# Cross-attention on one core: Wq and Wk in 512-byte runs turned by VectorE, the product G over 64 rows, and the first group's A in two halves

## The chip, the cores and the metric

The kernel runs on one core of one Trainium2 chip. The metric is the device time of one execution in microseconds. Four runs of the kernel before took 289.02 to 289.76 us, median 289.47.

## The reference

Sixteen images of 256 tokens attend to sixteen texts of 77 tokens, with 8 heads of 256 columns; everything is float32.

```python
# x (16,256,256), c (16,77,192); Wq (256,2048), Wk and Wv (192,2048), Wo (2048,256)
Q, K, V = heads(x @ Wq), heads(c @ Wk), heads(c @ Wv)
score = Q @ K.T / sqrt(256)           # masked keys get -inf
ctx = softmax(score) @ V
out = merge(ctx) @ Wo + x
y = (out - mean(out)) * rsqrt(var(out) + eps) * gamma + beta
```

## The kernel before, in words

The kernel never forms Q, K or V. For each head it multiplies the weights first: G = Wk·Wqᵀ (192 by 256) and U = Wv·Wo (192 by 256). The scores of an image are then x·A with A = Gᵀ·cᵀ, and the values are c·U. The 192 rows of c and of G are kept as 128 rows (cA, gA) and 64 rows (cB, gB, stored on both halves of the partitions, so that two matmuls over 64 rows can run on the two halves of TensorE's rows).

The order is written out by hand: the five engines each run their instructions in the order in which the program lists them. Loads go through SP's queue; the order of the program gives every load after the eighth a wait for the load eight before it. Up to the first scores the stages on TensorE are:

- ten idle transposes (L467), then the 22 transposes of ctx (`c_sb`, 11 blocks of 112 rows) at L475, evacuated in turn by ScalarE and VectorE (`evacuate`, L133 to L138) into cA and cB, with a copy of cB by GpSimd (L486). `vr` is set to zero at L490.
- for each of 8 heads: four transposes of Wq and four of Wk (L507, tiles p_wqT and p_wkT), evacuated to wqT and wkT, and then G (pg, L543): two matmuls over 128 rows, each of them two instructions in the profile, scaled into gA by L551. The transposes of head h+1 are issued ahead of G of head h.
- after four heads the last 64 rows of G for two pairs of heads (ph, L524), scaled into gB (L532, L534).
- A of the first group of four images (`prepare_a(0, ...)`), in two halves of four heads after all of G: part A with cA (L182), part B with cB (L196); in the second half part B comes ahead. Each half fills all eight PSUM banks. VectorE turns Wv in place meanwhile (L568).
- U (pu, L584, over 64 rows in pairs; pw, L602), then the values of the last 13 keys of all images (pr, L256 and L266).
- the scores of the first image (ps, L295), and from there a loop over the images.

The loads on SP come in this order: ctx in three pieces (L442); for each head a piece of Wq and of Wk (L445, L446), 256 columns of each row, so runs of 1024 bytes; Wv in sixteen loads (L454), each of 32 partitions with runs of 512 bytes from rows 8192 bytes apart; Wo (L456), whose tile takes the place of Wq's; the mask (L457); x in 256-byte runs to be turned (xT, L153, turned at L160); and x itself (xg, L129), whose tiles take the place of wqT and wkT. At L348 VectorE turns 32 by 32 blocks of the probabilities out of place.

Of the kernel before, what the change touches and what calls it, by code (L numbers as in the profile page):

```python
# [15 lines left out]
P = 128  # L16
# [28 lines left out]
def kernel(  # L45
# [16 lines left out]
    LP = DL // 2  # L62
# [34 lines left out]
    gA = const.tile([P, H, DI], F32, tag="gA", name="gA")  # L97
    gB = const.tile([P, NF, DI], F32, tag="gB", name="gB")
# [25 lines left out]
    def half(i):  # L124
        return slice(i * LB, (i + 1) * LB)
# [39 lines left out]
    def prepare_a(g, pairs, B_first=False):  # L165


        if 0 in pairs:
            a_of[g] = in_two("a", [P, 2, GB, H, S2], g)
        parts = [(2 * n + i, dc) for n in pairs for dc in range(2) for i in range(2)]  # L170
# [19 lines left out]
        def part_B():  # L190
            if B_first:
                banks.extend(ring_of(parts))
            for j in range(0, len(parts), 2):
                for i in range(NM):
                    for k, (h, dc) in enumerate(parts[j : j + 2]):
                        nc.tensor.matmul(  # L196
                            flat(banks[j + k][i * BK : (i + 1) * BK]),
                            gB[half(k), h // 2, cols(dc, i)],
                            flat(cB[half(k), batches, :]),
                            start=B_first,  # L200
                            stop=not B_first,
                        )
# [229 lines left out]
    with tc.tile_pool(name="wonce", bufs=1) as wp:  # L432
        c_sb = wp.tile([CR, NCR, DL], F32, tag="c", name="c_sb")
        wq_r = wq.rearrange("(t p) f -> p t f", p=P)
        wk_r = wk.rearrange("(t p) f -> p t f", p=LP)

        warm = wp.tile([P, 1], F32, tag="warm", name="warm")
        nc.scalar.activation(warm, eps, AF.Exp)
        wq_all = wp.tile([P, NF, 2, 2 * D], F32, tag="w128", name="wq_all")
        wk_all = wp.tile([LP, NF, 2, 2 * D], F32, tag="w96", name="wk_all")  # L440
        for lo, hi in ((0, 2), (2, 6), (6, NCR)):
            nc.sync.dma_start(c_sb[:, lo:hi, :], c_rows[:, lo:hi, :])  # L442
        for h in range(H):
            here, cols = slice(h % 2 * D, (h % 2 + 1) * D), slice(h * D, (h + 1) * D)
            nc.sync.dma_start(wq_all[:, h // 2, :, here], wq_r[:, :, cols])  # L445
            nc.sync.dma_start(wk_all[:, h // 2, :, here], wk_r[:, :, cols])  # L446
# [17 lines left out]

        def keep_busy(n):
            for i in range(n):
                nc.tensor.transpose(idle, ident, ident)  # L467

        keep_busy(10)
        for r in range(0, NCR, 2):  # L470
            n = min(2, NCR - r)
            pc = ps_mm.tile([P, 4, P], F32, tag="mm", name=f"pc_{r}")
            for lc in range(2):
                for j in range(n):
                    nc.tensor.transpose(  # L475
                        pc[:, 2 * lc + j, :CR],
                        c_sb[:, r + j, lc * LB : lc * LB + P],
                        ident[:CR, :CR],
                    )
            rows = slice(r * CR, (r + n) * CR)  # L480
            evacuate(flat(cA)[:, rows].rearrange("p (j m) -> p j m", m=CR), pc[:, :n, :CR])
            evacuate(
                flat(cB)[LB:, rows].rearrange("p (j m) -> p j m", m=CR),
                pc[LB:, 2 : 2 + n, :CR],
            )
            nc.gpsimd.tensor_copy(flat(cB)[:LB, rows], flat(cB)[LB:, rows])  # L486
        nc.gpsimd.tensor_copy(cRA, cA[:, :, KM:])
        nc.gpsimd.tensor_copy(cRB, cB[:, :, KM:])

        nc.gpsimd.memset(vr, 0.0)  # L490
# [3 lines left out]
            const.tile([P, H // 2, 2, DI], F32, tag=f"xg{i}", name=f"wqT_{i}") for i in range(2)  # L494
        ]
        wkT_of = [
            const.tile([P, H // 2, 2, DL], F32, tag=f"xg{i + 2}", name=f"wkT_{i}") for i in range(2)
        ]
        wqT = [wqT_of[h * 2 // H][:, h % (H // 2)] for h in range(H)]
        wkT = [wkT_of[h * 2 // H][:, h % (H // 2)] for h in range(H)]  # L500

        def turn_weight(dst, w_all, rows, h, tag):
            pt = ps_mm.tile([P, 4, P], F32, tag="mm", name=f"p_{tag}_{h}")
            for dc in range(2):
                for r in range(2):
                    lo = h % 2 * D + dc * P
                    nc.tensor.transpose(  # L507
                        pt[:, 2 * dc + r, :rows],
                        w_all[:, h // 2, r, lo : lo + P],
                        ident[:rows, :rows],  # L510
                    )
            evacuate(dst.rearrange("p a (r n) -> p (a r) n", r=2), pt[:, :, :rows])

        def turn_qk(h):
            turn_weight(wqT[h], wq_all, P, h, "wqT")
            turn_weight(wkT[h], wk_all, LP, h, "wkT")

        def rest_of_g(pairs):

            for n in pairs:  # L520
                pg = ps_mm.tile([P, DI], F32, tag="mm", name=f"ph_{n}")
                for dc in range(2):
                    for i in range(2):
                        nc.tensor.matmul(  # L524
                            pg[half(i)],
                            wkT[2 * n + i][:, dc, P:],
                            wqT[2 * n + i][:, dc, :],
                            start=(dc == 0),
                            stop=(dc == 1),
                        )  # L530
                if n % 2:
                    nc.scalar.mul(gB[:, n, :], pg, D ** -0.5)  # L532
                else:
                    nc.vector.tensor_scalar(gB[:, n, :], pg, D ** -0.5, None, ALU.mult)  # L534

        turn_qk(0)
        for h in range(H):
            if h + 1 < H:
                turn_qk(h + 1)
            if h % 2 == 0:  # L540
                pg = ps_mm.tile([P, 2, DI], F32, tag="mm", name=f"pg_{h}")
            for dc in range(2):
                nc.tensor.matmul(  # L543
                    pg[:, h % 2, :],
                    wkT[h][:, dc, :P],
                    wqT[h][:, dc, :],
                    start=(dc == 0),
                    stop=(dc == 1),
                )
            if h % 2:  # L550
                nc.scalar.mul(gA[:, h - 1 : h + 1, :], pg, D ** -0.5)  # L551
            if h % (H // 2) == H // 2 - 1:
                rest_of_g(range((h - 2) // 2, (h + 1) // 2))
        for g in range(NG):
            load_x(g)
            if g == 0:
                nc.sync.dma_start(gam, gamma.partition_broadcast(P))
                nc.sync.dma_start(bet, beta.partition_broadcast(P))

        for n in range(0, NF, 2):  # L560
            part_A, part_B, copies = prepare_a(0, (n, n + 1), B_first=(n > 0))
            for part in (part_A, part_B)[:: -1 if n else 1]:
                part()
            for dst, src in copies():
                evacuate(dst, src)
            for a in range(n, n + 2):
                blocks = wvT[:, a].rearrange("p m (c n) -> p m n c", n=4)
                nc.vector.transpose(blocks, blocks)  # L568
# [5 lines left out]


        def wv_part(a, e, n):
            return flat(wvT[half(e), a]).rearrange("p (l n) -> p n l", n=4)[:, n]

        for a in range(NF):
            if a % 2 == 0:  # L580
                pu = [ps_mm.tile([P, 2, DI], F32, tag="mm", name=f"pu_{a}_{e}") for e in range(2)]
            for n in range(4):
                for e in range(2):
                    nc.tensor.matmul(  # L584
                        pu[e][:, a % 2, :],
                        wv_part(a, e, n)[:, :P],
                        wo_all[half(e), a, n, :],
                        start=(n == 0),
                        stop=(n == 3),
                    )  # L590
            if a % 2:
                for e in range(2):
                    evacuate(
                        uA[:, e, :, a - 1 : a + 1].rearrange("p n a c -> p a n c"),
                        pu[e].rearrange("p a (n c) -> p a n c", c=BK),
                    )
        for pair in range(0, NF, 2):
            pw = [ps_mm.tile([P, DI], F32, tag="mm", name=f"pw_{pair}_{e}") for e in range(2)]
            for n in range(4):
                for i in range(2):  # L600
                    for e in range(2):
                        nc.tensor.matmul(  # L602
                            pw[e][half(i)],
                            wv_part(pair + i, e, n)[:, P:],
# [124 lines left out]
```

## Time and profile before

| | |
|---|---|
| median of four runs | 289.47 us |
| the profiled execution | 289.28 us |
| its span, first to last instruction | 287.1 us |
| start of the first scores (L295) | 60.45 us |
| TensorE busy, share of the span | 278.1 us, 97% |
| VectorE, ScalarE, GpSimd busy | 212.9, 118.6, 119.5 us |
| moved by DMA | 22.50 MB |

A row of digits in the profile cuts the span into 40 slices of 7.2 us; a digit is the busy share of a slice in tenths. The chain of work that ended last is followed back from the last instruction; each of its pieces has a start, a length and a source. Stretches of time show the busy time of each engine, the clock granted to TensorE, the mean busy share of the 16 DMA engines, and GB/s.

### The profile page before, as it was taken

How to read it: one execution, taken by the hardware profiler on the slowest of the kernel's cores; microseconds unless marked ns; L12 is line 12 of the kernel's file. 1: busy time of each engine (PE TensorE's matmuls, PEld its weight loads, DVE VectorE, ACT ScalarE, POOL GpSimd, SP SyncE). 2: the span in 40 equal slices, each digit the busy share in tenths (PEclk: the TensorE clock that was granted, in tenths of full speed). 3: DMA queues.
4: the chain of work that ended last, by engine and by line, in shares of the span. 5: the costliest groups of instructions: out<-in, count | busy, mean ns of one | idle time of the engine just before them, and what ended most of it. 6: DMA issues, size and time to landing. Idle time of an engine off the chain costs nothing.

```text
span 287.1 us, 11524 instructions
## 1 busy us (share of the span) xinstructions
PE 278.1 (97%) x5216; PEld 184.1 (64%) x5216; DVE 212.9 (74%) x419; ACT 118.6 (41%) x205; POOL 119.5 (42%) x150
## 2 busy tenths in 40 slices
PE   7999999999999999999999999999999999999990
PEld 6976569894666565656575757575757467576550
DVE  1422482765858798989797989897979898898884
ACT  3443222123253535353535353535353534635541
POOL 2700060804534334343334342434342527658584
PEclk9999999999999999999999999999999999999997
DMA  7998999990000101910101019000000000010112
GB/s 201 263 247 223 338 178 286 300 130 8 2 3 2 40 5 38 149 39 2 39 6 39 2 36 151 31 13 25 16 21 23 15 28 17 24 41 1 41 39 73
DMA packets 34673, 22.50 MB, mean 78 GB/s; under 512 B 17648, under 2 KB 33984, under 8 KB 34624
## 3 DMA queue, kind: packets, MB, share of 16 engines
q1 hardware_dynamic: 34624, 21.77, 32.7%
q8 instruction: 41, 0.67, 1.0%
q14 instruction: 8, 0.07, 0.1%
HBM read 17.57 MB, written 4.19 MB: 76 GB/s over the span
## 4 chain that ended last, share of the span: by engine, by line
PE 92%; DMA 2%; DVE 2%; POOL 2%; ACT 0%; issue 0%; POOLq 0%; SPq 0%
PE ps L295 23%; PE po L360 22%; PE pa L182 12%; PE pv L223 10%; PE pa L196 6%; PE pv L234 6%; PE pu L584 3%; PE pg L543 3%; PE pr L256 2%; DMA c_sb<-in_ctx_dram 2%; PE p_wqT L507 1%; PE ph L524 1%; PE pw L602 1%; PE pr L266 1%; PE p_wkT L507 1%; PE pc L475 1%
## 5 line engine op out<-in xcount | busy, mean ns | idle before, releaser
L317 POOL TENSOR_TENSOR s<-s,top 128x616 f32<-128x616 f32 x32 | 39.0, 1218 | 90.8 <-DVE top L316 86.4
L295 PE MATMUL ps<-a,xT 128*32 128x154 f32 x2048 | 70.0, 294 | 0.0
L295 PEld LDWEIGHTS ps<-a,xT 128*32 128x32 f32 x2048 | 66.4, 110 | 3.6 <-issue 0.8
L338 POOL TENSOR_TENSOR p<-e,rden 128x512 f32<-128x512 f32 x64 | 50.1, 802 | 31.8 <-ACT a L667 27.0
L360 PE MATMUL po<-vw,pT 128*32 128x256 f32 x1024 | 61.5, 380 | 0.0
L360 PEld LDWEIGHTS po<-vw,pT 128*32 128x32 f32 x1024 | 31.7, 110 | 28.2 <-issue 5.5
L330 DVE TENSOR_REDUCE den<-e 128x8 f32<-128x616 f32 x32 | 25.3, 790 | 23.7 <-ACT e L324 23.7
L182 PE MATMUL pa<-cA,gA 128*32 128x308 f32 x512 | 35.8, 423 | 0.0
L324 ACT ACTIVATE e<-s 128x616 f32<-128x616 f32 x32 | 23.0, 718 | 28.8 <-POOL s L317 28.7
L665 ACT COPY vw<-pv 128x512 f32<-128x512 f32 x32 | 18.6, 581 | 36.1 <-PE pv L234 36.1
L309 DVE TENSOR_TENSOR s<-ps,bias 128x308 f32<-128x308 f32 x64 | 27.8, 465 | 4.1 <-PE ps L295 4.1
L223 PE MATMUL pv<-uA,cA 128*32 128x512 f32 x256 | 30.4, 592 | 0.0
L182 PEld LDWEIGHTS pa<-cA,gA 128*32 128x32 f32 x512 | 16.4, 110 | 21.0 <-issue 6.6
L417 DVE SCALAR_TENSOR_TENSOR xg<-xg,rstd,bet 128x256 f32<-128x256 f32 x25 | 27.9, 1116 | 0.9
L385 ACT ACTIVATE std<-mv,eps 128x2 f32<-128x2 f32 (+1 forms) x17 | 5.0, 296 | 55.0 <-DVE mv L377 54.3
L348 DVE STREAM_TRANSPOSE pT<-p 128x640 f32<-128x640 f32 x32 | 25.0, 810 | 2.5 <-POOL p L338 2.5
L316 DVE TENSOR_REDUCE top<-s 128x8 f32<-128x616 f32 x32 | 25.4, 795 | 1.1
L360 PE MATMUL po<-vr,pT 128*32 128x256 f32 x256 | 19.7, 379 | 0.0
L385 ACT ACT_TABLE_LOAD x15 | 19.2, 1283 | 0.3
L196 PE MATMUL pa<-cB,gB 64*32 64x308 f32 x512 | 19.3, 419 | 0.0
L324 ACT ACT_TABLE_LOAD x14 | 18.0, 1283 | 0.2
L234 PE MATMUL pv<-uB,cB 64*32 64x512 f32 x256 | 17.4, 601 | 0.0
(73 smaller groups left out, 284.5 us busy)
## 6 DMA issues: line engine op xcount, KB each, us to landing
xT<-in_x_dram SPq DMA_DIRECT2D x16, 256.0 KB, 6.7
xg<-in_x_dram SPq DMA_DIRECT2D x4, 1024.0 KB, 11.4
out_dram<-xg SPq DMA_DIRECT2D x15, 256.0 KB, 2.3
wq_all<-in_L_xattn_Wq_dram SPq DMA_DIRECT2D x8, 256.0 KB, 6.9
wo_all<-in_L_xattn_Wo_dram SPq DMA_DIRECT2D x4, 512.0 KB, 5.5
wk_all<-in_L_xattn_Wk_dram SPq DMA_DIRECT2D x8, 192.0 KB, 6.9
wvT<-in_L_xattn_Wv_dram SPq DMA_DIRECT2D x16, 96.0 KB, 3.0
bias<-in_mask_BxS_if_dram SPq DMA_DIRECT2D x1, 616.0 KB, 9.7
```

Source lines behind the costliest of these rows:

```text
L182: nc.tensor.matmul(flat(o[i * BK : (i + 1) * BK]), gA[:, h, cols(dc, i)], flat(cA[:, batches, :]), start=not B_first, stop=B_first,)
L196: nc.tensor.matmul(flat(banks[j + k][i * BK : (i + 1) * BK]), gB[half(k), h // 2, cols(dc, i)], flat(cB[half(k), batches, :]), start=B_fir ...
L223: nc.tensor.matmul(pv[k][i * BK : (i + 1) * BK], cA[:, b, k * BK : (k + 1) * BK], uA[:, :, :, i], start=True, stop=False,)
L234: nc.tensor.matmul(pv[k][i * BK : (i + 1) * BK], cB[half(k), b, k * BK : (k + 1) * BK], uB[half(k), :, :, i], start=False, stop=True,)
L295: nc.tensor.matmul(ps[m // 2][i * BK : (i + 1) * BK, m % 2 * 2 * S2 : (m % 2 + 1) * 2 * S2], xT_of[g][:, j * NM + m, dc], flat(a_of[g][:, ...
L309: nc.vector.tensor_tensor(s[:, a * H // 2 : (a + 1) * H // 2], ps[a][:, : H // 2 * S2].rearrange("p (h k) -> p h k", k=S2), bias[:, b, :]. ...
L316: nc.vector.tensor_reduce(top, s, AX.X, ALU.max)
L317: nc.gpsimd.tensor_tensor(s, s, top.unsqueeze(2).to_broadcast([P, H, S2]), ALU.subtract)
L324: nc.scalar.activation(e, s_of.pop(t), AF.Exp)
L338: nc.gpsimd.tensor_tensor(part, e_mh[:, :, :, keys], rden_mh.unsqueeze(3).to_broadcast(list(part.shape)), ALU.mult,)
L360: nc.tensor.matmul(po[i * BK : (i + 1) * BK], pT[:, n, i], vw_of[b][:, n // 2, n % 2, :] if n < NF else vr[:, b, :], start=(n == 0), stop= ...
L417: nc.vector.scalar_tensor_tensor(y, y, rstd, bet, ALU.mult, ALU.add)
```

## The change

Wq and Wk come in four blocks of two heads. Each block is eight loads of 32 partitions with runs of 512 bytes, in the form that Wv has already: partition 32·i + r holds, for each 32-row block m of the weight, row r of column piece i. Wk of the first block is issued on ScalarE's queue, ahead of its table load, all others on SP. The first three blocks of ctx are loaded after two blocks of weights, the other eight after all four.

VectorE turns each block of 32 by 32 out of place (eight instructions in all), and the result holds 64 columns of one head on each half of the partitions for each of four steps n. TensorE has no transposes of Wq and Wk. G runs over 64 rows, two heads at once on the two halves, through functions that U shares: `of_pair` for the first 128 rows of G or U, `rest_of_pairs` for the last 64. gB has a new order of heads, and `prepare_a` picks its heads to match.

The order on TensorE becomes: 28 idle transposes; G of block 0; 6 transposes of ctx; G of block 1 and the rest of G for both; A of the first four heads; the other 16 transposes of ctx; G of blocks 2 and 3; A of the other heads, now with part A ahead in both halves; then U as before. The loads of x (xg) and gamma and beta are listed after the second part of G, in the same place on SP's queue as before, behind xT.

```diff
-        parts = [(2 * n + i, dc) for n in pairs for dc in range(2) for i in range(2)]
+        parts = [
+            (u // 2 * 4 + 2 * i + u % 2, dc) for u in places for dc in range(2) for i in range(2)
+        ]
...
-                            gB[half(k), h // 2, cols(dc, i)],
+                            gB[half(k), h // 4 * 2 + h % 2, cols(dc, i)],
...
+        wq_nat = wp.tile([P, NF, DI // BK, P], F32, tag="w128", name="wq_nat")
+        wk_nat = wp.tile([P, NF, NL, P], F32, tag="w96", name="wk_nat")
+        wq_blocks = wq.rearrange("(m r) (a i f) -> a i r m f", r=BK, a=NF, i=NM)
+        wk_blocks = wk.rearrange("(m r) (a i f) -> a i r m f", r=BK, a=NF, i=NM)
+
+        def load_qk(a, queues):
+            for queue, nat, blocks in zip(queues, (wk_nat, wq_nat), (wk_blocks, wq_blocks)):
+                for i in range(NM):
+                    queue.dma_start(nat[i * BK : (i + 1) * BK, a], blocks[a, i])
...
+        first = -(-GB * S2 // CR)
+        load_qk(0, (nc.scalar, nc.sync))
...
-        for lo, hi in ((0, 2), (2, 6), (6, NCR)):
-            nc.sync.dma_start(c_sb[:, lo:hi, :], c_rows[:, lo:hi, :])
-        for h in range(H):
-            here, cols = slice(h % 2 * D, (h % 2 + 1) * D), slice(h * D, (h + 1) * D)
-            nc.sync.dma_start(wq_all[:, h // 2, :, here], wq_r[:, :, cols])
-            nc.sync.dma_start(wk_all[:, h // 2, :, here], wk_r[:, :, cols])
+        load_qk(1, (nc.sync, nc.sync))
+        load_c(0, first)
+        load_qk(2, (nc.sync, nc.sync))
+        load_qk(3, (nc.sync, nc.sync))
+        load_c(first, NCR)
...
-        keep_busy(10)
+        for i in range(28):
+            nc.tensor.transpose(idle, ident, ident)
...
+        def turn_qk(a):
+            for nat, of in ((wk_nat, wkT_of), (wq_nat, wqT_of)):
+                nc.vector.transpose(
+                    of[a // 2][:, a % 2].rearrange("p n (m r) -> p m n r", r=BK),
+                    nat[:, a].rearrange("p m (n c) -> p m n c", c=BK),
+                )
...
+        def of_pair(out, a, weight, moving):
+
             for n in range(4):
                 for e in range(2):
                     nc.tensor.matmul(
+                        out[e][:, a % 2, :],
+                        weight(a, e, n)[:, :P],
+                        moving(a, e, n),
                         start=(n == 0),
                         stop=(n == 3),
                     )
...
+        turn_qk(0)
+        turn_qk(1)
+        for j in range(NF // 2):
+            pg = two_banks("pg", j)
+            of_pair(pg, 2 * j, wk_part, wq_part)
+            if j == 0:
+                turn_c(0, first)
+            of_pair(pg, 2 * j + 1, wk_part, wq_part)
             for e in range(2):
+                nc.scalar.mul(gA_of[:, j, e], pg[e], D ** -0.5)
+            for e, ph in enumerate(rest_of_pairs(j, wk_part, wq_part, "ph")):
+                nc.vector.tensor_scalar(gB[:, 2 * j + e, :], ph, D ** -0.5, None, ALU.mult)
+            if j == 0:
+                turn_qk(2)
+            else:
+                turn_v(0)
+                turn_v(1)
+                for g in range(NG):
+                    load_x(g)
...
+            part_A, part_B, copies = prepare_a(0, (2 * j, 2 * j + 1))
+            part_A()
+            part_B()
+            for i, (dst, src) in enumerate(copies()):
+                evacuate(dst, src)
+                if j == 0 and i == 3:
+                    turn_qk(3)
+            if j == 0:
+                turn_c(first, NCR)
+                nc.gpsimd.tensor_copy(cRA, cA[:, :, KM:])
+                nc.gpsimd.tensor_copy(cRB, cB[:, :, KM:])
+                nc.gpsimd.memset(vr, 0.0)
+        turn_v(2)
+        turn_v(3)
```

More of the change, by code (lines that the diff above doesn't have):

```diff
@@ L61 @@
     S2, DL = c.shape[1], c.shape[2]
-    LP = DL // 2
     LB = DL - P
@@ L160, in transpose_x, with prepare_a @@
         nc.vector.transpose(cols, cols)
-    def prepare_a(g, pairs, B_first=False):
-        if 0 in pairs:
+    def prepare_a(g, places, B_first=False):
+        if 0 in places:
             a_of[g] = in_two("a", [P, 2, GB, H, S2], g)
-        parts = [(2 * n + i, dc) for n in pairs for dc in range(2) for i in range(2)]
+        parts = [
+            (u // 2 * 4 + 2 * i + u % 2, dc) for u in places for dc in range(2) for i in range(2)
+        ]
         batches = slice(g * GB, (g + 1) * GB)
@@ L433, with load_c @@
         c_sb = wp.tile([CR, NCR, DL], F32, tag="c", name="c_sb")
-        wq_r = wq.rearrange("(t p) f -> p t f", p=P)
-        wk_r = wk.rearrange("(t p) f -> p t f", p=LP)
+        wq_nat = wp.tile([P, NF, DI // BK, P], F32, tag="w128", name="wq_nat")
[6 more added lines that the diff above has]
+                    queue.dma_start(nat[i * BK : (i + 1) * BK, a], blocks[a, i])
+        def load_c(lo, hi):
+            nc.sync.dma_start(c_sb[:, lo:hi, :], c_rows[:, lo:hi, :])
+        first = -(-GB * S2 // CR)
+        load_qk(0, (nc.scalar, nc.sync))
         warm = wp.tile([P, 1], F32, tag="warm", name="warm")
         nc.scalar.activation(warm, eps, AF.Exp)
-        wq_all = wp.tile([P, NF, 2, 2 * D], F32, tag="w128", name="wq_all")
-        wk_all = wp.tile([LP, NF, 2, 2 * D], F32, tag="w96", name="wk_all")
-        for lo, hi in ((0, 2), (2, 6), (6, NCR)):
-            nc.sync.dma_start(c_sb[:, lo:hi, :], c_rows[:, lo:hi, :])
-        for h in range(H):
-            here, cols = slice(h % 2 * D, (h % 2 + 1) * D), slice(h * D, (h + 1) * D)
-            nc.sync.dma_start(wq_all[:, h // 2, :, here], wq_r[:, :, cols])
-            nc.sync.dma_start(wk_all[:, h // 2, :, here], wk_r[:, :, cols])
+        load_qk(1, (nc.sync, nc.sync))
[3 more added lines that the diff above has]
+        load_c(first, NCR)
         wvT = wp.tile([P, NF, NL, P], F32, tag="wvT", name="wvT")
@@ L463 @@
         idle = ps_mm.tile([P, P], F32, tag="mm", name="idle")
-        def keep_busy(n):
-            for i in range(n):
-                nc.tensor.transpose(idle, ident, ident)
-        keep_busy(10)
[L470 to L486, printed above, removed]
@@ L487 @@
-        nc.gpsimd.tensor_copy(cRA, cA[:, :, KM:])
-        nc.gpsimd.tensor_copy(cRB, cB[:, :, KM:])
-        nc.gpsimd.memset(vr, 0.0)
+        for i in range(28):
+            nc.tensor.transpose(idle, ident, ident)
         wqT_of = [
-            const.tile([P, H // 2, 2, DI], F32, tag=f"xg{i}", name=f"wqT_{i}") for i in range(2)
+            const.tile([P, 2, 4, DI], F32, tag=f"xg{i}", name=f"wqT_{i}") for i in range(2)
         ]
         wkT_of = [
-            const.tile([P, H // 2, 2, DL], F32, tag=f"xg{i + 2}", name=f"wkT_{i}") for i in range(2)
+            const.tile([P, 2, 4, DL], F32, tag=f"xg{i + 2}", name=f"wkT_{i}") for i in range(2)
@@ L498 @@
         ]
[L499 to L529, printed above, removed]
-                        )
[L531 to L548, printed above, removed]
-                )
[L550 to L568, printed above, removed]
@@ L572 @@
-        nc.gpsimd.tensor_scalar(bias_f, bias_f.bitcast(I32), 0.0, -MASKED, ALU.is_equal, ALU.mult)
[L576 to L581, printed above, removed]
+        def turn_qk(a):
[4 more added lines that the diff above has]
+                )
@@ new lines, in turn_c @@
+        def turn_c(lo, hi):
+            for r in range(lo, hi, 2):
+                n = min(2, hi - r)
+                pc = ps_mm.tile([P, 4, P], F32, tag="mm", name=f"pc_{r}")
+                for lc in range(2):
+                    for j in range(n):
+                        nc.tensor.transpose(
+                            pc[:, 2 * lc + j, :CR],
+                            c_sb[:, r + j, lc * LB : lc * LB + P],
+                            ident[:CR, :CR],
+                        )
+                rows = slice(r * CR, (r + n) * CR)
+                evacuate(flat(cA)[:, rows].rearrange("p (j m) -> p j m", m=CR), pc[:, :n, :CR])
+                evacuate(
+                    flat(cB)[LB:, rows].rearrange("p (j m) -> p j m", m=CR),
+                    pc[LB:, 2 : 2 + n, :CR],
+                )
+                nc.gpsimd.tensor_copy(flat(cB)[:LB, rows], flat(cB)[LB:, rows])
@@ L582, with turn_v @@
+        def turn_v(a):
+            blocks = wvT[:, a].rearrange("p m (c n) -> p m n c", n=4)
+            nc.vector.transpose(blocks, blocks)
+        def of_pair(out, a, weight, moving):
             for n in range(4):
@@ L584 @@
                     nc.tensor.matmul(
-                        pu[e][:, a % 2, :],
-                        wv_part(a, e, n)[:, :P],
-                        wo_all[half(e), a, n, :],
+                        out[e][:, a % 2, :],
+                        weight(a, e, n)[:, :P],
+                        moving(a, e, n),
                         start=(n == 0),
@@ L590, with rest_of_pairs @@
                     )
[L591 to L598, printed above, removed]
+        def rest_of_pairs(j, weight, moving, name):
+            banks = [ps_mm.tile([P, DI], F32, tag="mm", name=f"{name}_{j}_{e}") for e in range(2)]
             for n in range(4):
@@ L602 @@
                         nc.tensor.matmul(
-                            pw[e][half(i)],
-                            wv_part(pair + i, e, n)[:, P:],
-                            wo_all[half(e), pair + i, n, :],
+                            banks[e][half(i)],
+                            weight(2 * j + i, e, n)[:, P:],
+                            moving(2 * j + i, e, n),
                             start=(n == 0),
@@ L608, with two_banks, wq_part, wk_part @@
                         )
-            for e in range(2):
+            return banks
+        def two_banks(name, j):
+            return [ps_mm.tile([P, 2, DI], F32, tag="mm", name=f"{name}_{j}_{e}") for e in range(2)]
+        def wq_part(a, e, n):
+            return wqT_of[a // 2][half(e), a % 2, n]
+        def wk_part(a, e, n):
+            return wkT_of[a // 2][half(e), a % 2, n]
+        def wv_part(a, e, n):
+            return flat(wvT[half(e), a]).rearrange("p (l n) -> p n l", n=4)[:, n]
@@ new lines, in wo_part @@
+        def wo_part(a, e, n):
+            return wo_all[half(e), a, n, :]
+        gA_of = gA.rearrange("p (j i e) d -> p j e i d", i=2, e=2)
+        turn_qk(0)
[6 more added lines that the diff above has]
+            of_pair(pg, 2 * j + 1, wk_part, wq_part)
+            for e in range(2):
+                nc.scalar.mul(gA_of[:, j, e], pg[e], D ** -0.5)
[8 more added lines that the diff above has]
+                    load_x(g)
+                    if g == 0:
+                        nc.sync.dma_start(gam, gamma.partition_broadcast(P))
+                        nc.sync.dma_start(bet, beta.partition_broadcast(P))
+            part_A, part_B, copies = prepare_a(0, (2 * j, 2 * j + 1))
[10 more added lines that the diff above has]
+                nc.gpsimd.memset(vr, 0.0)
@@ new lines @@
+        turn_v(2)
+        turn_v(3)
+        nc.gpsimd.tensor_scalar(bias_f, bias_f.bitcast(I32), 0.0, -MASKED, ALU.is_equal, ALU.mult)
+        for j in range(NF // 2):
+            pu = two_banks("pu", j)
+            for a in range(2 * j, 2 * j + 2):
+                of_pair(pu, a, wv_part, wo_part)
+            for e in range(2):
+                evacuate(
+                    uA[:, e, :, 2 * j : 2 * j + 2].rearrange("p n a c -> p a n c"),
+                    pu[e].rearrange("p a (n c) -> p a n c", c=BK),
+                )
@@ L610 @@
+        for j in range(NF // 2):
+            for e, pw in enumerate(rest_of_pairs(j, wv_part, wo_part, "pw")):
                 for i, engine in enumerate((nc.scalar.copy, nc.vector.tensor_copy)):
-                    here, there = uB[half(i), e, :, pair + i], uB[half(1 - i), e, :, pair + i]
-                    engine(here, pw[e][half(i)].rearrange("p (n c) -> p n c", c=BK))
+                    a = 2 * j + i
+                    here, there = uB[half(i), e, :, a], uB[half(1 - i), e, :, a]
+                    engine(here, pw[half(i)].rearrange("p (n c) -> p n c", c=BK))
```

## The prediction, as it was put on record

> **What bounds the kernel now.** I read the page's parts 1 and 2 first, then the chain of work that ended last in order of time, then the loads in stretches of one microsecond.
>
> ```profile
> span 287.1 us, 11524 instructions
> PE   7999999999999999999999999999999999999990
> DMA  7998999990000101910101019000000000010112
> ```
>
> TensorE is full from the second slice to the last but one. The loads are full as well, but only for the first nine slices (65 us). All edits lie before the first scores (L295), which start at 60.45 us, so that moment is what I forecast. What follows it, 226.7 us of span, has the same instructions in both programs.
>
> ```profile
> 1.66 5.07 DMA c_sb<-in_ctx_dram
> 6.77 2.13 PE pc L475 x10
> 8.90 0.85 PE p_wqT L507 x4
> ...
> 13.93 0.44 PE p_wqT L507 x4
> 14.36 0.33 PE p_wkT L507 x4
> 14.69 0.89 PE pg L543 x4
> ...
> 25.21 1.88 PE ph L524 x16
> 27.09 4.29 PE pa L182 x64
> 31.38 4.31 PE pa L196 x128
> 35.68 4.28 PE pa L182 x64
> 39.97 7.77 PE pu L584 x64
> 47.74 3.68 PE pw L602 x64
> ...
> 60.45 4.33 PE ps L295 x128
> ```
>
> The columns are start, length, and what it was. From 6.77 us to 60.45 us the chain is TensorE without a gap: 53.7 us. The eight pairs of p_wqT and p_wkT groups, added over the chain, are 4.28 + 2.96 = 7.24 us. Note the pace: the first four p_wqT take 0.85 us, every four after 10.6 us take 0.44.
>
> **How the loads run.** The issue instructions on SP wait, from the ninth load on, for the load eight issues earlier, so the start times of issues are landing times. The ctx rows (0.946 MB) and the first piece of Wq (0.262 MB) had been moved at 6.4 us by the sum of the stretches, and the issue that waits for that piece came at 8.04 us: a load lands 1.7 us after its last byte moved.
>
> ```profile
> 14.00:15.00 1.00, 1.00 (x11) 0.95 (x10) 0.27 (x1) 1.00 (x2) 0.18 (x1) 1.00 1.12 260
> 19.00:20.00 1.00, 1.00 (x11) 0.94 (x10) 0.00 (x0) 0.63 (x2) 0.00 (x0) 1.00 1.22 215
> 20.00:21.00 1.00, 1.00 (x8) 0.85 (x7) 0.56 (x1) 0.34 (x1) 0.00 (x0) 1.00 1.26 204
> 21.00:22.00 1.00, 1.00 (x10) 0.96 (x9) 0.25 (x1) 0.59 (x1) 0.00 (x0) 1.00 1.21 221
> ```
>
> The last three columns are the clock, the load engines' busy share and GB/s. Until 19 us Wq and Wk come in 1024-byte runs at about 265 GB/s. From 19.2 us only Wv is under way, in 512-byte runs from rows 8 KB apart, exactly the form that the change gives Wq and Wk. The engines are full (1.2) and move 213 GB/s, the mean of the three.
>
> [...]
>
> **Part by part.** *Removed:* 64 transposes on TensorE (−7.24 us) and their 16 evacuations on ScalarE and VectorE, beside it. *G:* 16 matmuls over 128 rows (two instructions each, 32 in all: 8 groups of 0.89 = 7.2 us) become 32 over 64 rows, in pairs on the two halves of the rows. Pairs of 64 rows run side by side: L266 does 32 in 3.01 us, L256 16 of 128 rows in 3.01. So G costs 7.2 again if weight loads hide. In L584, the same shape, 64 instructions take 7.77; its loads read every fourth element (326 ns) and fill the weight queue. The new weights lie side by side as in L266 (187 ns). Bounds 0 and +0.6 us; I take 0, nearest L266. Rest of G: 3.76 now, 3.68 in the form of L602. *A of group 0:* the same 64 + 64 matmuls, 12.9 us, in two halves of 4.28 + 2.15 = 6.43 us. *ctx transposes:* 22, now before 8.9 us at 0.19 each; 16 of them move behind the first half of A. At the pace after 10.6 us (0.11 for 128 rows, 0.083 for 96) they cost about 0.10 each, 2.2 in all.
>
> *Added on VectorE:* eight block transposes, out of place in the manner of L348: 797 ns for 640 columns, and 670 for 512 on L160, so about 1.0 ns a column and 0.16 us: 0.93 us for Wk (768 columns), 1.18 for Wq (1024). At the other end stands the transpose of Wv, in place with a stride, 1.63 us for 768; that would be 1.63 and 2.17. L348 moves runs of 32 as the new ones do, so I take its row.
>
> *Moved on the queues:* four loads of Wk go to ScalarE's queue ahead of its table load, which is needed by nobody before 13 us. On SP ctx goes behind half of the weights, its last eight rows behind all of them. The load of Wo waits for the last transpose of Wq in both orders, with the mask, xT and x queued behind it.
>
> **The sum, in microseconds of the span.** Data starts moving at 2.0 us as now. One block (two heads) is 0.524 MB of Wq and 0.393 of Wk, 0.917 in all: 4.3 us at 213 GB/s. Block 0 lands at 2.0 + 4.3 + 1.7 = 8.0 (Wk, on its own ring, at 7.4), is turned at 9.5, and G of it runs 9.5 to 11.3. Block 1 lands at 12.3, is turned at 13.5. The first three ctx rows (0.258 MB, 1.0 us at 270) land at 13.25: TensorE waits 1.9 us here, a new wait; 6 transposes to 13.85. G of block 1 to 15.65, rest of G to 17.5, first half of A to 23.9. Blocks 2 and 3 land at 17.6 and 21.9, and VectorE turns them at 18.4 to 20.5 and 23.4 to 25.5, beside A. The last ctx rows (0.688 MB, 2.55 us) land at 20.2 + 2.55 + 1.7 = 24.4, a second wait, 0.5 us. From there it is all TensorE: 1.6 (ctx) + 3.6 + 1.84 (G) + 6.43 (A) + 7.77 + 3.68 (U) + 9.03 (L256, L266) = 33.9. The scores start at 58.3 instead of 60.45: **−2.1 us**.
>
> So of the 7.24 saved some 5 go to the later start and to ctx: today the first weights are needed at 8.7 and their blocks follow singly, and half of ctx is turned before.
>
> Covers I checked: Wv is moved by 30.1 and lands at 31.8, turned from 32.2; Wo starts landing at 33.5, U starts at 37.9; the last two turns of Wv end 0.1 us before they are needed, as now. The mask lands near 40 for GpSimd's 4.4 us; xT near 48 for VectorE at 52. If Wo's start slipped by over 4 us, U would be late by the rest. Memset of vr (3.5 us) moves to 30 on GpSimd; nobody waits.
>
> **Rivals.** *First, slower:* 512-byte runs move slower than Wv's did, as Wq and Wk come four blocks deep through two rings. The last ctx rows then set the end: landing + 33.9, and landing = 2.0 + 3.67/pace + 3.5 + 1.7. It decides from 190 GB/s on (landing 26.5, no gain). The far row is xT, 256-byte runs, 142 to 160 GB/s at 37 to 40 us: landing 31.7, +5.2 us. At 175, nearer the row, +1.7: 291.0. Against it: 204 was the lowest whole microsecond, which gives −1.3.
>
> *Second, slow TensorE:* now it runs at half pace until 10.6, though the clock column shows 1.00 and it has worked since 6.8 without a gap. In the changed program the 28 idle transposes end near 7.3, then come waits to 9.5 and from 11.3 to 13.25. If half pace lasts to block 1, its G ends at 17.9 instead of 15.65; the sum is −0.3. If it ends at 13.4, about 3.9 us after work resumed, as in the row of now, most is hidden in the wait: −1.5. So 287.8 to 289.0.
>
> [...]
>
> *Third, the loads keep the pace of 1024-byte runs* (265): block 1 is turned at 11.8, ctx is no wait, A's first half ends at 22.3, scores start at 56.2: −4.2, 285.1. For it: single 512-byte loads at 24 us moved 215 GB/s at a busy share of only 0.76.
>
> That the change does not do what it says is excluded by the order of its instructions: no transposes of Wq and Wk are left on TensorE, eight are on VectorE. Slow transposes (the row of Wv) would turn block 1 at 15.0 and give −1.4, within the forecast's own range.
>
> **How the numbers follow.** The profiled execution took 289.28 us (span 287.1), 0.2 below the median of 289.47; 289.28 − 2.1 = 287.2. About 0.2% (0.6 us) is what a measurement here can tell from no change. Chances: forecast 0.55 (285.6 to 288.4, from 235 GB/s down to slow transposes or 204), slower loads 0.17, half pace 0.13, full pace of loads 0.15. Faster: 0.54 + 0.05 + 0.15, less 0.04 for mishaps that I do not see = 0.70; slower 0.16; same 0.14. The range 285.0 to 290.0 reaches to the third rival and through the second into the first.
>
> **What would show it.** In the changed profile: no waits of TensorE but for the first block (to 9.5), the first ctx rows (to 13.3) and the last (to 24.4); block transposes at 0.93 and 1.18; G groups of 1.8 per block; 213 GB/s from 3 to 20 us; scores from 58.3. I am wrong if TensorE waits for block 2 or 3, for Wo or for xT, or if a stage after the scores changes its length.

## The result, and the profile after

Nothing changed that can be measured. The changed kernel took 289.46 us in the median of 38 runs, the kernel before 289.38 in 62; the ratio is 1.0006, 95% interval 0.9995 to 1.0018. The profiled execution took 289.63 us, its span 287.8. The forecast was 287.2, with 285.0 to 290.0 as range.

From the page of the changed kernel, its span and two rows of the 40 slices:

```profile
span 287.8 us, 11561 instructions
PE   6599999999999999999999999999999999999990
PEclk9779999999999999999999999999999999999997
```

TensorE is less busy in the first two slices (6 and 5, where the kernel before has 7 and 9), and the clock granted to it falls below full speed in the second and third slice. Before, that row was

```profile
PEclk9999999999999999999999999999999999999997
```

TensorE in the changed kernel in order of time (start, length, what, and in brackets the idle time ahead with what ended it):

```profile
1.34 4.88 PE L478 MATMUL idle<-ident 128*128 128x128 f32 x28 [1.34 <-POOL ident masks.py:199]
10.13 2.49 PE L524 MATMUL pg<-wqT,wkT 64*128 64x256 f32 x16 [3.91 <-DVE wqT L490]
13.00 1.38 PE L501 MATMUL pc<-ident,c_sb 112*128 112x112 f32 x6 [0.38 <-DMA c_sb<-in_ctx_dram]
14.31 3.79 PE L524 MATMUL pg<-wqT,wkT 64*128 64x256 f32 x16
18.02 2.08 PE L538 MATMUL ph<-wqT,wkT 64*64 64x256 f32 x32
20.03 4.36 PE L184 MATMUL pa<-cA,gA 128*32 128x308 f32 x64
24.32 2.30 PE L198 MATMUL pa<-cB,gB 64*32 64x308 f32 x64
26.79 1.72 PE L501 MATMUL pc<-ident,c_sb 112*128 112x112 f32 x16 [0.17 <-DMA c_sb<-in_ctx_dram]
28.45 3.72 PE L524 MATMUL pg<-wqT,wkT 64*128 64x256 f32 x32
```

The 64 transposes are gone. But G of block 1 takes 3.79 us, while G of blocks 2 and 3 together takes 3.72: block 1 ran at half pace. And the transposes of the last ctx rows start at 26.79, after a wait of only 0.17 us. The first scores start at 61.06 us instead of 60.45; after them come 226.7 us of span in both kernels. So nearly the whole story lies ahead of 26.8 us.

The same kernel in stretches (start:end, length, busy time of TensorE, its weight loads, VectorE, ScalarE, GpSimd, then clock, busy share of the DMA engines, GB/s), and three pieces of its chain:

```profile
3.00:9.00 6.00, 3.22 (x22) 2.98 (x20) 1.03 (x2) 1.13 (x2) 0.00 (x0) 1.00 1.23 191
11.00:12.00 1.00, 1.00 (x12) 0.81 (x8) 0.00 (x0) 0.00 (x0) 0.00 (x0) 0.75 1.12 230
14.00:15.00 1.00, 1.00 (x7) 0.64 (x7) 0.58 (x2) 0.60 (x2) 0.04 (x1) 0.50 1.23 204
18.00:19.00 1.00, 1.00 (x18) 0.73 (x20) 0.00 (x0) 0.87 (x2) 0.00 (x0) 0.84 1.25 205
13.00:21.00 8.00, 8.00 (x70) 5.29 (x74) 1.93 (x6) 1.68 (x4) 0.59 (x2) 0.67 1.23 200
```

```profile
18.16 8.49 DMA c_sb<-in_ctx_dram
26.79 1.72 PE pc L501 x16
...
61.06 4.32 PE ps L297 x128
```

The clock stands at 0.50 from 11.5 (the expectation below has 11.7) to 18.3 us. The weights come at 191 GB/s from 3 to 9 us and at 200 from 13 to 21, with the DMA engines full (1.23), not at 213, and the last ctx rows land 8.49 us after their issue, at 26.65. So two things hold TensorE, and in this execution by chance to the same moment: its work, part of it at half pace, ends at 26.62, and ctx lands at 26.65. Theory 3 in the experiments says that either of the two is enough by itself. Its rivals: the half pace alone (theory 1), or the late ctx rows alone (theory 2).

### The profile page after: what moved, and what is told of

Its sections match the earlier page's. It is cut to its first block, busy times and chain, and to the rows that moved or that the text cites. A ratio compares the mean times of both kernels' runs of the same rounds, so it can differ in the third digit from the quotient of the medians.

```text
span 287.8 us, 11561 instructions
## 1 busy us (share of the span) xinstructions
PE 274.7 (95%) x5234; PEld 179.6 (62%) x5234; DVE 217.0 (75%) x421; ACT 113.1 (39%) x195; POOL 119.1 (41%) x150
## 4 chain that ended last, share of the span: by engine, by line
PE 85%; DMA 8%; DVE 2%; POOL 1%; issue 1%; ACTq 0%; ACT 0%; SPq 0%; POOLq 0%
PE ps L297 23%; PE po L362 22%; PE pa L184 10%; PE pv L225 10%; PE pv L236 6%; PE pa L198 5%; DMA wk_nat<-in_L_xattn_Wk_dram 5%; DMA c_sb<-in_ctx_dram 3%; PE pu L524 3%; PE pr L258 2%; PE pw L538 1%; PE pg L524 1%; PE pr L268 1%; PE ph L538 1%; PE pc L501 1%; POOL xg L413 1%
```

## The experiments

Ratios are to the kernel before, run on the same chip; in brackets is the 95% interval.

**e1: TensorE kept busy through its waits.**

```diff
-        for i in range(28):
-            nc.tensor.transpose(idle, ident, ident)
+
+        def keep_busy(n):
+            for i in range(n):
+                nc.tensor.transpose(idle, ident, ident)
+
+        keep_busy(58)
...
             if j == 0:
+                keep_busy(8)
                 turn_c(0, first)
```

> TensorE is kept busy through its two waits: 58 idle transposes ahead of block 0 instead of 28, and 8 more between block 0 and the first ctx rows. Theory 1 (the half pace from 11.7 to 18.3 us alone took the gain): the scores start near 58.6 instead of 61.06, time 287.0. Theory 2 (the last ctx rows alone, landing at 26.66) and theory 3 (either of the two holds TensorE by itself, until the same moment): full pace, the first half of A ends near 24, but TensorE then waits some 2.5 us for ctx, scores at 60.8, time 289.2, no change beyond 0.2%.

Measured: 289.50 us, ratio 0.9998 (0.9972 to 1.0024). TensorE in order of time:

```profile
14.13 2.00 PE L528 MATMUL pg<-wqT,wkT 64*128 64x256 f32 x16
...
22.23 2.30 PE L198 MATMUL pa<-cB,gB 64*32 64x308 f32 x64
26.56 1.72 PE L505 MATMUL pc<-ident,c_sb 112*128 112x112 f32 x16 [2.02 <-DMA c_sb<-in_ctx_dram]
```

G of block 1 is back at full pace (2.00 us) and the first half of A ends 2.1 us earlier, at 24.5. All of it turns into a wait of 2.02 us for ctx. So the late ctx rows are enough by themselves, and theory 1 falls.

**e2: the last ctx rows turned later**, after G of blocks 2 and 3; TensorE's waits are left as they were.

```diff
-            if j == 0:
-                turn_c(first, NCR)
-                nc.gpsimd.tensor_copy(cRA, cA[:, :, KM:])
...
             else:
+                turn_c(first, NCR)
+                nc.gpsimd.tensor_copy(cRA, cA[:, :, KM:])
...
                 turn_v(0)
```

> The 16 transposes of the last ctx rows move behind G of blocks 2 and 3, to just before the second half of A; their load stays. Theory 2 (late ctx alone): the wait and all that hangs on it go, time 287.0. Theory 1 and theory 3: the first half of A still ends at 26.5 after the half pace, only the wait of 0.17 us goes, scores at 60.9, time 289.2 to 289.5.

Measured: 288.26 us, ratio 0.9943 (0.9917 to 0.9969). The gain is 1.2 us by the medians and 1.6 by the ratio: more than half of the forecast, where theory 3 expected none, and less than the whole of theory 2. TensorE in this run, and two stretches:

```profile
10.31 3.07 PE L524 MATMUL pg<-wqT,wkT 64*128 64x256 f32 x16 [4.30 <-DVE wqT L490]
13.57 1.22 PE L501 MATMUL pc<-ident,c_sb 112*128 112x112 f32 x6 [0.19 <-DMA c_sb<-in_ctx_dram]
14.72 2.00 PE L524 MATMUL pg<-wqT,wkT 64*128 64x256 f32 x16
```

```profile
11.00:12.00 1.00, 1.00 (x10) 0.81 (x8) 0.11 (x1) 0.00 (x0) 0.00 (x0) 0.54 1.12 198
14.00:15.00 1.00, 1.00 (x8) 0.85 (x8) 0.01 (x1) 0.39 (x2) 0.00 (x0) 0.75 1.23 206
```

Here the half pace began during block 0 and was over before block 1: it lasted from 11.1 to 14.5 us, 3.4 us against 6.8 in the trace of the change. The mean clock of a run tells the two apart, 0.983 for the longer and 0.990 for the shorter, while e1, which keeps the full clock through this stretch, has 0.995. With the ctx wait gone the time goes with it: the four runs of e2 with a mean clock of 0.979 to 0.983 took 288.6 us in the mean, the four at 0.989 and 0.990 took 287.7. In the changed kernel it matters less: 23 runs at 0.979 to 0.984 have a median of 289.73, 13 at 0.986 to 0.989 one of 289.26, and the two at 0.995 took 289.10 and 289.26. Without a half pace, then, the changed kernel still gains nothing; and with a long one e2 still gains something. Theory 3 is too strict: that the half pace alone takes the whole gain is not shown.

**e3: both edits together.**

> Both edits of the two runs beside it. All three theories but none other expect full pace and no ctx wait: first half of A to 23.8, G of blocks 2 and 3 to 27.4 with block 3 turned at 25.7, ctx to 31.0, second half of A to 37.5. Wo must land its first quarter by then (37.3 by my sum) and the mask's 4.4 us on GpSimd, which now end at 49.0, would hold the copies of uB by up to 0.7. Scores at 58.0 to 58.7, time 286.5 to 287.2. Theory 3 needs this run alone of the first three to be faster. If it stays at 289, something later than both is the bound.

Measured: 287.61 us, ratio 0.9920 (0.9895 to 0.9945). TensorE:

```profile
24.21 3.72 PE L528 MATMUL pg<-wqT,wkT 64*128 64x256 f32 x32
27.86 1.96 PE L542 MATMUL ph<-wqT,wkT 64*64 64x256 f32 x32
29.75 1.75 PE L505 MATMUL pc<-ident,c_sb 112*128 112x112 f32 x16
...
58.66 3.61 PE L297 MATMUL ps<-a,xT 128*32 128x154 f32 x104
```

No waits are left after 13.9 us, and the scores start at 58.66, 1.7 us ahead of the kernel before (60.38 in this view). The gain that was forecast is there once both holds are taken away: the ctx wait is worth 1.9 us (e1 against e3; 2.1 in the traces), the half pace 0.65 (e2 against e3; 0.6 in the traces). The second is small: the intervals of e2 and e3 overlap.

**e4: TensorE busy, the last ctx rows loaded ahead of blocks 2 and 3.**

```diff
         load_c(0, first)
+        load_c(first, NCR)
         load_qk(2, (nc.sync, nc.sync))
         load_qk(3, (nc.sync, nc.sync))
-        load_c(first, NCR)
```

> TensorE busy as in the first run, its order that of the change; the load of the last ctx rows goes ahead of the weights of blocks 2 and 3. The same bytes must land before block 3 can be used, 3.4 us later than the ctx rows were needed in the first run. Theory 3: ctx is there at 24, block 3 lands near 25.3 and is turned at 27.5, G of it starts then without or with a wait under 0.5; second half of A ends near 37.7, scores 58.2 to 58.8, time 286.6 to 287.3. Theory 1: as the first run, 287.0. If 512-byte loads as such bound the stage whatever their order, 289.

Measured: 287.33 us, ratio 0.9919 (0.9894 to 0.9944), scores at 58.94. The ctx rows were there when the first half of A ended (24.59). So it is the place of ctx on the queue, not the amount of data, that held TensorE.

**Why the loads are slow.** My row for them was Wv before the change, 213 GB/s, and I put the loss against 265 down to the 512-byte run. The runs e5 to e10 test that.

**e5: runs of 1024 bytes**, all else as in e1.

```diff
-        wq_blocks = wq.rearrange("(m r) (a i f) -> a i r m f", r=BK, a=NF, i=NM)
+        wq_blocks = wq.rearrange("(u m r) (a i f) -> a i u r m f", u=2, r=BK, a=NF, i=2)
...
-                    queue.dma_start(nat[i * BK : (i + 1) * BK, a], blocks[a, i])
+                    to = nat[i * BK : (i + 1) * BK, a].rearrange("p (m n) f -> p m (n f)", n=2)
+                    queue.dma_start(to, blocks[a, i // 2, i % 2])
```

> The first run (TensorE kept busy) with the same number of loads, bytes and partitions, but each load of Wq and Wk moves half as many runs of 1024 bytes instead of 512; the weights land at wrong places, so only its time is read. If the length of the run sets the pace: about 265 GB/s instead of 200 up to 18 us, the last ctx rows land near 22.5, block 1 is turned near 12.2, no wait for ctx after A, scores 57.0 to 58.0, time 285.5 to 286.5. If it is the form of 32 partitions to a load, the two rings or the issue that is slow, whatever the run: pace 200, ctx at 26.5, time 289.4.

Measured: 287.71 us, ratio 0.9944 (0.9924 to 0.9965). Stretches:

```profile
3.00:9.00 6.00, 6.00 (x43) 6.00 (x42) 1.37 (x2) 1.10 (x2) 0.00 (x0) 1.00 1.13 215
12.00:17.00 5.00, 5.00 (x60) 3.97 (x62) 1.73 (x3) 1.58 (x4) 0.59 (x2) 1.00 1.13 224
```

The pace rises by about a tenth, to 215 and 224 (192 and 210 in e1), and the last ctx rows are there at 24.5. It does not come near the 265 of the kernel before, whose runs are as long. Both of my readings missed; something besides the run's length costs more.

**e6: no load of Wv beside the last ctx rows.**

```diff
-        wvT = wp.tile([P, NF, NL, P], F32, tag="wvT", name="wvT")
+        wvT = wp.tile([P, NF, NL, P], F32, tag="w96", name="wvT")
```

> The first run (TensorE kept busy) with the tile of Wv laid where Wk's was, so that Wv's loads wait until VectorE has turned Wk of block 3 (about 25 us) and none of them is under way beside the last ctx rows. If the eight loads of Wv behind them hold these rows up, they land by 25.2 instead of 26.5 and TensorE's wait of 2.0 us falls to about 0.8; if not, 26.5 as before. Wv and Wo land up to 3 us later than in the first run, so U may wait for Wo: time between 288.5 and 290; what is read is the end of the wait for ctx.

Measured: 288.69 us, ratio 0.9975 (0.9952 to 0.9998). TensorE:

```profile
25.53 1.72 PE L505 MATMUL pc<-ident,c_sb 112*128 112x112 f32 x16 [0.89 <-DMA c_sb<-in_ctx_dram]
```

The rows land 1.0 us earlier than in e1, in one trace of each: here the loads issued behind these rows delayed their landing.

**e7: the kernel before, its loads of Wq and Wk split into 512-byte runs.**

```diff
-            nc.sync.dma_start(wq_all[:, h // 2, :, here], wq_r[:, :, cols])
-            nc.sync.dma_start(wk_all[:, h // 2, :, here], wk_r[:, :, cols])
+            for to, of in ((wq_all, wq_r), (wk_all, wk_r)):
+                for k in range(2):
+                    lo = h % 2 * D + k * P
+                    cols = slice(h * D + k * P, h * D + (k + 1) * P)
+                    nc.sync.dma_start(to[:, h // 2, :, lo : lo + P], of[:, :, cols])
```

> The kernel before with one part of the change alone: each load of Wq and Wk is split in two of half as many columns, so runs of 512 bytes and 32 loads, all else as it was. If the run's length sets the pace (about 200 GB/s in place of 265, 3.67 MB): the last head's weights land 4.5 us later, near 25.4, while TensorE turns them at 22.4 now; the start at 8.7 also slips by about 0.5. Scores 3 to 4 us later, time 292.4 to 293.4. If the run's length does not matter in the old form of 128 and 96 partitions: 289.4.

Measured: 289.42 us, ratio 1.0000 (0.9980 to 1.0019). A stretch, and the only wait of TensorE for weights:

```profile
6.00:11.00 5.00, 4.99 (x33) 4.52 (x32) 2.35 (x7) 2.58 (x7) 2.33 (x8) 1.00 1.21 258
```

```profile
23.23 0.39 PE L509 MATMUL p_wkT<-ident,wk_all 96*128 96x96 f32 x2 [0.28 <-DMA wk_all<-in_L_xattn_Wk_dram]
```

Here runs of 512 bytes moved at 258 GB/s, in loads that span 128 or 96 partitions, against about 265 in the runs of 1024 of the kernel before. So the run's length explains little; the other part of the new form, 32 partitions to a load, is suspect.

**e8: e3 with blocks 0 and 1 over two rings, dealt by partitions; e9: the same rings, dealt by weight.** Both have 52 and 4 idle transposes.

```diff
+        def load_halves(a):
+            for nat, blocks in ((wk_nat, wk_blocks), (wq_nat, wq_blocks)):
+                for i in range(2):
+                    for queue, k in ((nc.sync, i), (nc.scalar, i + 2)):
+                        queue.dma_start(nat[k * BK : (k + 1) * BK, a], blocks[a, k])
```

> The version with both edits (busy, ctx late), and the loads of blocks 0 and 1 dealt over two rings by partitions: SP takes partitions 0 to 63, ScalarE 64 to 127, so that loads to two different groups of 32 partitions are under way at once; 52 and 4 idle transposes instead of 58 and 8. If 32 partitions at a time are what makes these loads slow (200 GB/s, where the old form of 128 and 96 partitions moved the same 512-byte runs at 255): 240 or more from 3 to 9 us, block 1 turned near 12.4 instead of 13.7, scores near 57.6, time 286.4. If not: pace 200 as before, scores 58.6, time 287.5.

> The control beside it: also two rings for blocks 0 and 1, but dealt by weight (Wk on ScalarE, Wq on SP), both going through the groups of 32 partitions in step, as the change has it for block 0. If a second ring by itself helps, it is as fast as its neighbour; if the partitions matter, it stays at 200 GB/s, block 1 turned near 13.5, scores 58.5, time 287.4.

Measured: e8 285.82 us, ratio 0.9892 (0.9872 to 0.9912), scores at 57.14; e9 286.88, ratio 0.9924 (0.9903 to 0.9944), scores at 58.14. The same stretch of e8, then of e9:

```profile
3.00:9.00 6.00, 6.00 (x45) 6.00 (x44) 2.85 (x3) 1.49 (x2) 0.00 (x0) 1.00 0.94 251
```

```profile
3.00:9.00 6.00, 6.00 (x46) 5.83 (x44) 1.38 (x2) 1.49 (x2) 0.00 (x0) 1.00 1.23 198
```

Same bytes, same runs, same rings: 198 GB/s with the engines full when both rings go through the groups of 32 partitions in step, 251 with engines not even full (0.94) when one ring writes partitions 0 to 63 and the other 64 to 127. Block 1 is turned at 12.0 us in e8 and at 13.3 in e9. e8 beats both kernels, by 1.1%.

**e10: one ring, the groups in the order 0, 2, 1, 3**, else e1.

```diff
-                for i in range(NM):
+                for i in (0, 2, 1, 3):
```

> The first run (TensorE kept busy) with the loads of each weight block in the order of partition groups 0, 2, 1, 3 instead of 0, 1, 2, 3, on the rings of the change. If it is enough that consecutive loads of one ring go to different halves of the partitions: about 225 GB/s or more from 13 to 21 us, the last ctx rows land near 24.5 instead of 26.5, time 287.5. If a ring works through one load after the other, so that only 32 partitions are written at a time whatever the order: 200 GB/s, ctx at 26.5, time 289.4.

Measured: 287.75 us, ratio 0.9940 (0.9907 to 0.9974). A stretch of e1, then the same of e10:

```profile
13.00:21.00 8.00, 7.73 (x104) 4.77 (x106) 4.13 (x7) 1.58 (x4) 0.59 (x2) 1.00 1.21 201
13.00:21.00 8.00, 8.00 (x110) 4.95 (x114) 3.56 (x7) 1.59 (x4) 0.59 (x2) 1.00 0.89 204
```

```profile
24.90 1.73 PE L505 MATMUL pc<-ident,c_sb 112*128 112x112 f32 x16 [0.79 <-DMA c_sb<-in_ctx_dram]
```

The order alone brings the ctx rows 1.7 us forward. The engines' busy share falls from 1.21 in e1 to 0.89, so they are no longer what limits the loads. The GB/s of the whole stretch hardly rise (201 to 204), but in the slice of the page from 7.2 to 14.3 us the pace is higher than in e1 (231 against 208). Later the loads wait for SP: it issues four of them in 1.8 to 2.2 us, and from 15.25 us on four in 3.15, as the program lets each wait for the landing of a load eight before it. That this is the limit there was not tested by itself.

## Why the prediction was wrong

- *What bounds the kernel* held: TensorE from the first weights on, and what the change cost or gained lies ahead of the scores.
- *Costs on TensorE* held. G takes 3.65 us for two blocks on the chain (forecast 3.6) with weight loads of 187 ns, the rest of G 1.89 (1.84), 16 ctx transposes 1.72 (1.6). The block transposes take 0.97 and 1.20 us (0.93 and 1.18). Block 1 was turned at 13.5, as forecast; block 0 at 10.1 instead of 9.5.
- *The landing of the last ctx rows failed: 26.65 instead of 24.4.* This is the step of the sum that failed. It took the pace of Wv, "exactly the form that the change gives Wq and Wk", 213 GB/s, and nothing for the loads behind. The pace was 200 with the engines full, which puts the four blocks about 1.1 us later; another 1.0 us came from Wv's loads behind these rows (e6). I had put the gap to 265 down to the 512-byte run, which e7 (258) refutes for loads over 128 and 96 partitions; over 32, longer runs brought a tenth (e5). The first rival's sum, landing + 33.9, stood: 60.6 against 61.06; its limit of no gain, a landing at 26.5, is where the run came out. That is in part luck: the rival reached it with 190 GB/s and nothing for Wv, the run with 200 and Wv.
- *The half pace came, and the sum had left it out.* I let TensorE wait 2.2 us. The idle transposes themselves came to full pace and ended at 6.2 instead of 7.3, block 0 was turned at 10.1, so the wait was 3.9 us; the clock fell at 11.5, and G of block 1 took 3.79 us where e1 has 2.00. The second rival's price for that was near: it had this G end at 17.9, and it ended at 18.1. It found ctx landed at 24.4, though, and so kept a gain of 0.3.
- *The two were set up as rivals, though they can happen together.* They lie side by side ahead of the same instruction, so their costs do not add: the later one counts. The late ctx rows take the whole gain by themselves, which is why e1 showed nothing. The half pace by itself takes 0.65 us in the median, which is why e2 showed only a part and both edits together the whole (e3). In the profiled execution of the change it lasted long enough to hide the wait for ctx.

What four traces show of the half pace: waits of 3.9 and 4.3 us were followed by a clock of 0.50 (the change from 11.5 us, e2 from 11.1), and in e1 and e3, with waits of 0.4 there, it stayed at 1.00. How long a wait has to be for that, no run here shows.

What spoke against this change was something that I had not weighed: which partitions are written at one time. The runs show that it matters: 198 GB/s with both rings in step within one half of the partitions (e9), 251 with one ring to each half (e8), both from 3 to 9 us. Not every row keeps to the lower figure: in e5 the same order of groups as in the change moved 224. Why the partitions matter, no run here shows.

What stays open: how much of the tenth in e5 belongs to the run's length and how much to the number of runs; why Wv moved at 213 before and the weights at 191 to 200 now; and why the traces of e2, e3 and e4 show some 0.5 us more behind the start of the scores than the other kernels.

## What to carry to other kernels

A load that fills 32 partitions was not as fast here as one that fills 128 or 96: 201 GB/s (e1) against 258 (e7), both in runs of 512 bytes. So look at which partitions are being written at one time, and try neighbouring loads (e10), or two rings (e8: 251 against 198 in e9), on different halves. When work is taken off the busiest engine at the start of a kernel, list every arrival that its next instructions need; two late ones side by side cost the later, and removing one by itself may show little or nothing (e1). After waits of 3.9 and 4.3 us TensorE here did part of its next work at half pace, and with the wait filled it did not (e1, e3): fill such a wait up to the moment of arrival.

## What was not expected of the hardware

A ctx load of 672 KB held SP's queue for 2.9 us, because the program lets the eighth load behind it wait for its landing; the DMA engines fell to a busy share of 0.24 at 27 us and the loads of Wv and Wo slipped: Wo was issued from 31.95 us, before the change from 26.15. It cost nothing here, since TensorE needed Wo only at 40.5. The clock column shows 1.00 in the first microseconds, while the idle transposes before about 4.5 us take 0.21 us each, twice as long as those after (0.11); the drop at 11.5 it does show.
